# Causal masks of the score maxima in an attention and mixture-of-experts kernel: from TensorE to GpSimd, by way of copies in SBUF

## The chip, the core and the metric

The kernel runs on one core of a Trainium2 chip. The metric is the time of one execution on the device in microseconds (us), the median of several runs. A smaller time is better. All lines (L472 and the like) are lines of the kernel before, unless the text says that they are of the changed kernel.

## The reference, cut to what matters

Eight batches of 256 tokens with 256 features go through an attention layer (32 query heads of 8 features, in groups of 4 over 8 key heads, rotary positions, causal) and then through a mixture of experts with 8 routed experts, of which each token takes 2, and 2 shared experts. Both have a layer norm before and after, and a residual. The part that the change touches is the causal softmax:

```
scores = einsum('bkgtd,bksd->bkgts', qg, k) / sqrt(hd)
scores = where(causal, scores, -inf)
attn   = softmax(scores, axis=-1)
ctx    = einsum('bkgts,bksd->bkgtd', attn, v)
```

A softmax subtracts the largest score of each query before the exponential. The kernel therefore computes the scores twice: once with the queries on the partitions, only to find the maxima, and a second time with the keys on the partitions, with the maxima subtracted inside the matmul, for the exponentials. The change concerns the first of these, the pass for the maxima.

## The kernel before, in words

A batch has two tiles of 128 tokens (tt = 0 and 1). For each batch the kernel normalises x, transposes it, projects it to queries, keys and values (`project`, L342), splits the rotated queries and keys into high and low parts on GpSimd (`split`, L379), and brings keys and queries into their transposed layouts through PSUM (`keysT`, L404, whose copy out of PSUM is L423 and L425; `queriesT`, L436). `keys_apart` (L427) then spreads the keys by DMA.

**The pass for the maxima** (`maxima_of` L450, `maxima` L461). With queries of tile tt on the partitions, the keys that can be seen are the first (tt+1)*128. A score tile in PSUM holds at most 512 columns: for tt = 0 there are ten tiles (eight of 3 heads x 128 columns, two of 2 query groups x 2 heads x 128), for tt = 1 sixteen of 512 columns (2 heads x 256, or 2 groups x 1 head x 256). Each score matmul (L472) is followed by a second one (L479) that adds the mask on the array: a bf16 identity as the weights, and as moving operand a bf16 triangle of 0 and -1e30, repeated for the heads, into the last 128 columns of each head, which are those on the diagonal. That is 32 score matmuls and 32 mask matmuls in a batch, 256 of each in all. VectorE then takes the negated maximum of each row out of PSUM (L486), 26 times in a batch, 208 in all. `split_shift` (L494) and `shiftT` (L501) split these maxima into two parts, transpose them, and send them by three DMAs (L516) into the extra rows of the queries.

**The second pass** (`weights_of`, L521) makes scores again (L524), ScalarE exponentiates them into one of nine buffers (`ex`, L531, L532), GpSimd zeroes the upper triangle of the diagonal tiles there (L534), and `values` (L545) multiplies with the values (L552). `softmaxed` (L564), `contextT` and `projected` follow, then the norms and the residual (L619 to L629).

**The experts.** `tokensT`, `logits`, `first_choice`, `second_choice`, `places`, `shares` and `scatter` (L645 to L764) choose two experts for each token. `scatter` issues four indirect DMAs from GpSimd for a batch (L754), each after a small multiplication (L748) that needs `den` (L714) from VectorE. The shared experts (`shared_gate_up` L802 with L780, `shared_down` L820 with L793) are spread through the attention as work for TensorE between the other matmuls. After the attention come the routed experts, block by block.

**The order of the work.** All of the attention is put on one line of time by hand: `at(when, step, ...)` (L299) gives each step a place in units of one batch, and the sorted list is issued in that order (L1200). Each engine works through its own instructions in that order. Batch b's maxima stand at b-0.98 and the following places, 0.032 apart (L1097 to L1103), batch b's second pass from b to b+0.98, and the projection of batch b+1 and the scatter of batch b-2 fall between the maxima of batch b: the maxima of tile 1 of batch b lie beside the `split`, `keysT` and `queriesT` of tile 1 of batch b+1 and the `scatter` of batch b-2.

**PSUM buffers.** Score tiles of both passes, gate-up and down tiles share five (`ps_mm`, L115). All transposes and small projections share two (`ps_tp`, L116), used in turn: a tile there can be written when the one two before it has been read.

Of the kernel before, what the change touches and what calls it, by code (L numbers as in the profile page):

```python
# [10 lines left out]
F32 = mybir.dt.float32  # L11
F32R = mybir.dt.float32r
BF16 = mybir.dt.bfloat16
I32 = mybir.dt.int32
AF = mybir.ActivationFunctionType
ALU = mybir.AluOpType
# [3 lines left out]
P = 128  # L20
EPS = 1e-5
NEG = -1e30
HD = 8
HB = 32
SHIFT = 96
SQ = 32
EB = 256
# [3 lines left out]
def attn_moe_kernel(  # L31
# [47 lines left out]
    nc = tc.nc  # L79
    B, T, D = x.shape  # L80
# [10 lines left out]
    ISC = IS // P  # L91
    G = 4
    NKV = NH // G
    NK = NKV * HD
    NC = NKV // G
    J = 3
    NS = -(-NKV // J)
# [5 lines left out]
    RW = 4  # L103
# [9 lines left out]
    small = ctx.enter_context(tc.tile_pool(name="small", bufs=4))  # L113
    shared_pool = ctx.enter_context(tc.tile_pool(name="shared", bufs=1))
    ps_mm = ctx.enter_context(tc.tile_pool(name="ps_mm", bufs=5, space=PSUM))  # L115
# [3 lines left out]
    aconst = early.enter_context(tc.tile_pool(name="aconst", bufs=1))  # L119
    work = early.enter_context(tc.tile_pool(name="work", bufs=2))  # L120
# [7 lines left out]
    NREG = -(-NSLOT // (16 * EB)) * 16  # L128
# [12 lines left out]
    for w, lo, n in ((wq, 0, D), (wk, D, NK), (wv, D + NK, NK)):  # L141
        nc.scalar.dma_start(
            out=wqkv[:, :, lo : lo + n], in_=w.rearrange("(k p) n -> p k n", p=P)
# [3 lines left out]
    for b in range(1, B):  # L147
# [9 lines left out]
    mask = aconst.tile([P, P], BF16, name="mask")  # L157
    nc.gpsimd.memset(mask, 0.0)
    nc.gpsimd.affine_select(
        out=mask,  # L160
        in_=mask,
        pattern=[[-1, P]],
        compare_op=ALU.is_ge,
        fill=NEG,
        base=0,
        channel_multiplier=1,
    )
    ident_b = aconst.tile([P, P], BF16, name="ident_b")
# [8 lines left out]
    for sign, base in ((1, 0), (-1, 1)):  # L177
        nc.gpsimd.affine_select(
            out=place1[SHIFT:P],
            in_=place1[SHIFT:P],  # L180
            pattern=[[-2 * sign, J], [0, 1]],
            compare_op=ALU.is_ge,
            fill=0.0,
            base=base,
            channel_multiplier=sign,
# [27 lines left out]
    def set_up_router():  # L213
        nonlocal order, ones, before, upto, region0, fills, blocks, cum, unused

        order = const.tile([P, NSEL], F32, name="order")
        for e in range(NSEL):
            nc.gpsimd.memset(order[:, e : e + 1], float(NSEL - e))


        ones = const.tile([P, P], BF16, name="ones")
        before = const.tile([P, P], BF16, name="before")
        nc.gpsimd.memset(ones, 1.0)
        nc.gpsimd.affine_select(
            out=before,
            in_=ones,
            pattern=[[1, P]],
            compare_op=ALU.is_gt,
            fill=0.0,
            base=0,  # L230
            channel_multiplier=-1,
        )
        upto = const.tile([P, 2 * NSEL, 2 * NSEL], F32, name="upto")
        nc.gpsimd.memset(upto, 1.0)
        nc.gpsimd.affine_select(
            out=upto,
            in_=upto,
            pattern=[[1, 2 * NSEL], [-1, 2 * NSEL]],
            compare_op=ALU.is_ge,
            fill=0.0,  # L240
            base=0,
            channel_multiplier=0,
        )

        def counter(name, *pattern, base=0):
            sizes = [n for _, n in pattern]
            i = const.tile([P, *sizes], I32, name=f"{name}_i")
            nc.gpsimd.iota(i, pattern=[*map(list, pattern)], base=base, channel_multiplier=0)
            f = const.tile([P, *sizes], F32, name=name)
            nc.vector.tensor_copy(f, i)  # L250
            return f

        region0 = counter("region0", (NTOK, NSEL))

        fills = counter("fills", (-P, 2), (EB, NTOK // EB - 1), base=EB + P)
        blocks = counter("blocks", (1, NBLK - NSEL))
        cum = const.tile([P, NT + 1, NSEL], BF16, name="cum")
        nc.vector.memset(cum[:, 0, :], 0.0)


        unused = aconst.tile([NREG, EB, RW], I32, name="unused")
        nc.gpsimd.memset(unused, 0)
        nc.gpsimd.iota(
            unused[:, :, 1], pattern=[[1, EB]], base=NTOK, channel_multiplier=0
        )
        nc.gpsimd.memset(records, 0)
        nc.gpsimd.iota(
            records[:, :, :, 0], pattern=[[P, NT], [0, 2]], base=0, channel_multiplier=1
        )
        nc.gpsimd.iota(  # L270
            records[:, :, :, 1], pattern=[[1, NT], [0, 2]], base=0, channel_multiplier=NT
        )
# [26 lines left out]
    def at(when, step, *args):  # L299
        timeline.append((when, len(timeline), step, args))  # L300

    held = {}
# [98 lines left out]
    def heads_in(c):  # L401
        return min(J, NKV - c * J)
# [46 lines left out]

    def maxima_of(b, tt):  # L450

        width = (tt + 1) * P
        for c in range(NS):
            per = min(512 // width, heads_in(c))
            for k0 in range(0, heads_in(c), per):
                nk = min(per, heads_in(c) - k0)
                ng = 512 // (nk * width)
                for g0 in range(0, G, ng):
                    yield c, c * J + k0, nk, g0, ng

    def maxima(b, tt, c, k0, nk, g0, ng):  # L461

        qA, kst = qAs[b % 3], ksts[b % 3]
        if ("nmx", b, tt) not in held:
            held["nmx", b, tt] = small.tile(
                [P, NKV, G], F32, tag="nmx", name=f"nmx{b}_{tt}", bufs=2
            )
        nmx = held["nmx", b, tt]
        width = (tt + 1) * P
        sc = ps_mm.tile([P, ng, nk, width], F32, tag="mm", name="sc")  # L470
        for g in range(ng):
            nc.tensor.matmul(  # L472
                sc[:, g, :, :],
                lhsT=qA[0:SHIFT, c * G + g0 + g, ts(tt, P)],
                rhs=kst[0:SHIFT, k0 : k0 + nk, 0:width],
                start=True,
                stop=False,
            )
            nc.tensor.matmul(  # L479
                sc[:, g, :, width - P :],  # L480
                lhsT=ident_b,
                rhs=mask.unsqueeze(1).to_broadcast([P, nk, P]),
                start=False,
                stop=True,
            )
        nc.vector.tensor_reduce(  # L486
            nmx[:, k0 : k0 + nk, g0 : g0 + ng].rearrange("p k g -> p g k"),
            sc,
            AX.X,
            ALU.max,  # L490
            negate=True,
        )

    def split_shift(b, tt):  # L494
        nmx = held.pop(("nmx", b, tt))
        nhl = small.tile([P, NKV, 2, G], F32R, tag="nhl", name=f"nhl{b}_{tt}", bufs=2)
        nc.vector.tensor_copy(nhl[:, :, 1, :], nmx)
        nc.vector.tensor_tensor(nhl[:, :, 0, :], nmx, nhl[:, :, 1, :], ALU.subtract)
        held["nhl", b, tt] = nhl
# [21 lines left out]
    def weights_of(b, kv, s, t):  # L521
# [8 lines left out]
        )  # L530
        e = work.tile([P, G, P], F32, tag="ex", name="ex", bufs=EX)  # L531
        nc.scalar.activation(e, sc, AF.Exp, scale=QSCALE)  # L532
# [31 lines left out]
    def softmaxed(b, c, t):  # L564

        avs = held.pop(("avs", b, c, t))
        if c == 0:
            held["cx", b, t] = work.tile([P, D], F32, tag="cx", name=f"cx{b}_{t}", bufs=4)
        cx = held["cx", b, t]
        pt = ps_tp.tile([P, G, G, 32], F32, tag="tp", name="pav")  # L570
        for g in range(G):
            nc.tensor.transpose(
                pt[:, g, :, :].rearrange("p j r -> p (j r)"), avs[:, ts(g, P)], ident
            )
        rs = small.tile([P, G, G], F32, tag="rs", name="rs")
        nc.vector.reciprocal(
            rs, pt[:, :, :, HD : HD + 1].rearrange("p g j x -> p g (j x)")
        )
        nc.vector.tensor_tensor(
            cx[:, ts(c, P)].rearrange("p (j g d) -> p g j d", j=G, g=G),  # L580
            pt[:, :, :, 0:HD],
            rs.unsqueeze(3).to_broadcast([P, G, G, HD]),
            ALU.mult,
        )
# [472 lines left out]
        )  # L1057


    EX = 9  # L1060
    at(0.6, clear_slots)
    at(0.7, clear_sums)
    for i in range(PIECES):
# [1 line left out]
    for i, a in enumerate((-2.2, -0.93, 0.03)):  # L1065
        at(a, clear_operands, i)
        at((-1.7, a, a)[i], set_ones, i)
        at((-1.97, -0.96, 0.02)[i], clear_values, i)
    at(0.5, set_up_router)
    at(-2.3, norm1, 0)  # L1070
    at(-2.3, normed1, 0)
# [10 lines left out]
    for b in range(B):  # L1082
# [14 lines left out]
        when = b - 0.98  # L1097
        for tt in range(TT):
            for m in maxima_of(b, tt):
                at(when, maxima, b, tt, *m)  # L1100
                when += 0.032
            at(when + 0.001, split_shift, b, tt)
            at(when + 0.07, shiftT, b, tt)  # L1103
        last = b == B - 1
        parts_of = [(c, t) for c in range(NC) for t in range(TT)]
        when, unit = b, 0.98 / (NC * 3 * G)
        if b == 0:
            parts_of.sort(key=lambda part: part[1])
            when, unit = -0.4, 0.04
        for c, t in parts_of:  # L1110
            if b == 0 and t > 0:
                when = max(when, 0)
# [222 lines left out]
```

## Time and profile before

| what | value |
|---|---|
| runs | 822.48, 825.74, 825.18 us; median 825.18 |
| the profiled execution | 821.22 us, its span 819.5 us, mean granted TensorE clock 0.975 |
| TensorE (PE) busy | 757.0 us, 3977 matmuls |
| VectorE (DVE) busy | 490.6 us |
| ScalarE (ACT) busy | 250.6 us |
| GpSimd (POOL) busy | 347.8 us |
| score matmuls L472 | 256, 99.5 us busy, mean 419 ns |
| mask matmuls L479 | 256, 73.2 us busy, mean 288 ns |
| maxima L486 | 208, 129.0 us busy, mean 641 ns |

PE is the row of the matmuls and PEld that of their weight loads, which overlap. Matmuls are pipelined: the row of one shows it from its start to its modelled end, and the next one starts before that end, so busy times of TensorE count the same moment twice and its cost is better read from the distance between the ends of neighbours. A matmul of f32 data with f32 weights stands in the trace as two records (a gate-up tile of four matmuls as x8), one of the types float32r or bf16 as one. The first 20 us set the kernel up, the attention lasts until about 500 us, and the routed experts take the rest.

### The profile page before, as it was taken

The page shows a single profiled execution, that of the slowest core. Times are in us where ns is not written, and L with a number is a line of the kernel's source. Part 1 is how long each engine was busy: PE and PEld are TensorE (multiplying, and loading weights), DVE is VectorE, ACT ScalarE, POOL GpSimd, SP SyncE. Part 2 cuts the span into 40 slices and gives each one's busy share as a digit, 9 for nine tenths or more (in the row PEclk, how much of TensorE's full clock was granted, in tenths as well). Part 3 has the DMA queues.
Part 4 walks back from the last instruction along what each step waited for, and adds up shares of the span by engine and source line. Part 5 has one row for each costly group of instructions (what it writes and reads, how often), then busy time and mean ns, then how long its engine had stood idle before and what let it go on. Part 6 is the DMA issues. An engine that isn't in the chain of part 4 may idle for free. (4 is left out here: it accounts for less than half of the span.)

```text
span 819.5 us, 11843 instructions
## 1 busy us (share of the span) xinstructions
PE 757.0 (92%) x3977; PEld 575.8 (70%) x3977; DVE 490.6 (60%) x1409; ACT 250.6 (31%) x550; POOL 347.8 (42%) x622
## 2 busy tenths in 40 slices
PE   4979799999999999999999998799999999999981
PEld 3535466766766766766766667688888888888961
DVE  5756777667667667667675636366564656442234
ACT  3554444234234334334334422021111111111213
POOL 4567545435435436436233432334233443443224
PEclk9899999999999999999999999899999999999986
DMA  5023300000000000000000005265655757577343
GB/s 155 6 85 90 89 16 16 7 22 16 8 23 16 7 21 16 8 22 16 7 22 3 19 8 203 52 229 157 203 163 179 225 158 228 167 220 279 57 118 102
DMA packets 30994, 70.41 MB, mean 86 GB/s; under 512 B 8544, under 2 KB 25440, under 8 KB 28240
## 3 DMA queue, kind: packets, MB, share of 16 engines
q1 hardware_dynamic: 19488, 54.23, 19.1%
q0 software_dynamic: 8128, 9.77, 6.4%
q10 hardware_dynamic: 3312, 5.60, 2.3%
q8 instruction: 33, 0.54, 0.3%
q14 instruction: 33, 0.27, 0.1%
HBM read 55.16 MB, written 11.80 MB: 82 GB/s over the span
## 5 line engine op out<-in xcount | busy, mean ns | idle before, releaser
L780 PE MATMUL gu<-xgT,w 128*128 128x256 f32 (+1 forms) x840 | 163.9, 354 | 1.0 <-ACT xgT L981 0.7
L780 PE MATMUL gu<-x2T,ws_sb 128*128 128x256 f32 x640 | 155.4, 390 | 3.9 <-PEq L1241 3.8
L780 PEld LDWEIGHTS gu<-xgT,w 128*128 128x128 f32 x840 | 144.5, 190 | 18.1 <-ACT xgT L981 1.0
L532 ACT ACTIVATE ex<-scT 128x512 f32<-128x512 f32 x192 | 113.6, 597 | 136.2 <-PE scT L524 123.7
L486 DVE TENSOR_REDUCE nmx<-sc 128x2 f32<-128x512 f32 (+2 forms) x208 | 129.0, 641 | 24.1 <-PE sc L479 23.8
L780 PEld LDWEIGHTS gu<-x2T,ws_sb 128*128 128x128 f32 x640 | 121.4, 195 | 26.1 <-issue 5.0
L534 POOL TENSOR_SCALAR_AFFINE_SELECT ex<-ex 128x512 f32<-128x512 f32 x128 | 81.1, 639 | 113.5 <-ACT ex L532 113.4
L1017 POOL DMA_INDIRECT sums<-yb,of x37 | 58.5, 1582 | 109.5 <-DVE yb L1016 71.7
L472 PE MATMUL sc<-kst,qA 96*128 96x512 f32 (+2 forms) x256 | 99.5, 419 | 0.7 <-issue 0.5
L524 PE MATMUL scT<-qA,kst 102*128 102x512 f32 x192 | 96.2, 509 | 1.8 <-DMA qA<-nm 1.8
L1006 ACT ACTIVATE sg<-gu 128x256 f32<-128x256 f32 (+1 forms) x105 | 37.6, 358 | 191.1 <-PE gu L780 177.8
L994 DVE STREAM_TRANSPOSE xgT<-xg 32x128 f32<-32x128 f32 x240 | 72.6, 303 | 29.9 <-DMA xg<-rows,of 21.1
L793 PE MATMUL po<-w,act 128*128 128x256 f32 x370 | 83.1, 379 | 0.0
L793 PE MATMUL po<-ws_sb,sact 128*128 128x256 f32 x320 | 74.6, 390 | 4.5 <-DVE sact L816 4.5
L793 PEld LDWEIGHTS po<-w,act 128*128 128x128 f32 x370 | 69.8, 190 | 9.2
L793 PEld LDWEIGHTS po<-ws_sb,sact 128*128 128x128 f32 x320 | 61.5, 195 | 18.2 <-DVE sact L816 4.9
L479 PE MATMUL sc<-mask,ident_b 128*128 128x256 bf16 (+2 forms) x256 | 73.2, 288 | 0.0
L1007 DVE TENSOR_TENSOR act<-sg,gu 128x256 f32<-128x256 f32 (+1 forms) x105 | 38.7, 387 | 56.3 <-ACT sg L1006 55.7
L815 DVE SCALAR_TENSOR_TENSOR th<-th,gu 128x256 f32<-128x256 f32 x70 | 29.3, 418 | 65.6 <-ACT th L814 65.6
L935 POOL DMA_INDIRECT xg<-rows,of x37 | 35.9, 970 | 62.4 <-DMA of<-slots 47.6
L472 PEld LDWEIGHTS sc<-kst,qA 96*128 96x128 f32 x256 | 50.3, 197 | 13.5 <-issue 3.6
L552 PE MATMUL av<-ex,v_aug 128*32 128x512 f32 x384 | 58.5, 605 | 1.3 <-POOL ex L534 1.3
(171 smaller groups left out, 839.9 us busy)
## 6 DMA issues: line engine op xcount, KB each, us to landing
w<-in_routed SPq DMA_DIRECT2D x21, 1920.0 KB
ws_sb<-in_shared ACTq DMA_DIRECT2D x8, 480.0 KB
xs<-in_x SPq DMA_DIRECT2D x8, 256.0 KB
rows<-x2n SPq DMA_DIRECT2D x8, 256.0 KB
acc<-sums SPq DMA_DIRECT2D x4, 512.0 KB
sums<-ya SPq DMA_DIRECT2D x14, 128.0 KB
kst<-kA SPq DMA_DIRECT2D x16, 96.0 KB
out<-acc SPq DMA_DIRECT2D x2, 512.0 KB
```

The costliest lines, as they stand in the source:

```text
L472: nc.tensor.matmul(sc[:, g, :, :], lhsT=qA[0:SHIFT, c * G + g0 + g, ts(tt, P)], rhs=kst[0:SHIFT, k0 : k0 + nk, 0:width], start=True, stop= ...
L479: nc.tensor.matmul(sc[:, g, :, width - P :], lhsT=ident_b, rhs=mask.unsqueeze(1).to_broadcast([P, nk, P]), start=False, stop=True,)
L486: nc.vector.tensor_reduce(nmx[:, k0 : k0 + nk, g0 : g0 + ng].rearrange("p k g -> p g k"), sc, AX.X, ALU.max, negate=True,)
L524: nc.tensor.matmul(sc, lhsT=ksts[b % 3][0:KR, kv, ts(s, P)], rhs=qAs[b % 3][0:KR, ts(kv // J, G), ts(t, P)], start=True, stop=True,)
L532: nc.scalar.activation(e, sc, AF.Exp, scale=QSCALE)
L534: nc.gpsimd.affine_select(out=e, in_=e, pattern=[[0, G], [1, P]], compare_op=ALU.is_ge, fill=0.0, base=0, channel_multiplier=-1,)
L552: nc.tensor.matmul(av[32 * j : 32 * j + 32, :], lhsT=v_aug[b % 3 * TT + s][:, c * G + j, :], rhs=e.rearrange("p g t -> p (g t)"), start=(s ...
L780: nc.tensor.matmul(gu[:, half, :], lhsT=m[:, k, ts(i, P)], rhs=xT[:, k, :], start=(k == 0), stop=(k == KC - 1),)
L793: nc.tensor.matmul(po, lhsT=act[:, k, ts(t, P)], rhs=d[:, k, :], start=(k == 0), stop=(k == ic - 1),)
L994: nc.vector.transpose(to[ts(j, SQ), :, :, ts(i, SQ)], of[ts(i, SQ), :, :, ts(j, SQ)])
L1007: nc.vector.tensor_tensor(act[:, i, :], sg, gu[:, 1, :], ALU.mult)
L1017: put = nc.gpsimd.indirect_dma_start(out=sums, out_offset=bass.IndirectOffsetOnAxis(ap=of[:, t, 1:2], axis=0), in_=y, in_offset=None, comp ...
```

## The change

For batches 0 and 1 the mask stays on the array. From batch 2 on (`BY_POOL = 2`) it leaves: the score tile of a diagonal block is copied by ScalarE from PSUM to one of five SBUF buffers (`sm`), GpSimd sets the upper triangle to -1e30 there with `affine_select`, and VectorE takes the maxima from SBUF. Score tiles are now always 128 keys wide for each head, for all batches; tile 1 has its off-diagonal block (kt = 0) and its diagonal block (kt = 1) in separate tiles, whose two maxima are combined by one more small VectorE instruction in `split_shift`. The places of the steps are new: tiles stand 0.026 apart (0.024 from batch 2 on), the select of a diagonal tile comes 0.03 and its maximum 0.07 after its matmul, and `split_shift` moves behind that. To make room in SBUF, `ex` has 8 buffers instead of 9 and `cx` 3 instead of 4, and the table `unused` takes the place of the buffer of the shared experts' activations, which is first written later.

```diff
-        unused = aconst.tile([NREG, EB, RW], I32, name="unused")
+        unused = shared_pool.tile([P, ISC, T], F32, tag="sact", name="unused")
+        unused = unused[0:NREG].rearrange("p i t -> p (i t)")[:, 0 : EB * RW].bitcast(I32)
...
     def maxima_of(b, tt):
-        width = (tt + 1) * P
-        for c in range(NS):
-            per = min(512 // width, heads_in(c))
-            for k0 in range(0, heads_in(c), per):
-                nk = min(per, heads_in(c) - k0)
-                ng = 512 // (nk * width)
+        for kt in range(tt + 1):
+            for c in range(NS):
+                nk = heads_in(c)
+                ng = 1 if kt == tt and b >= BY_POOL else 512 // (nk * P)
                 for g0 in range(0, G, ng):
-                    yield c, c * J + k0, nk, g0, ng
+                    yield kt, c, g0, ng
 
-    def maxima(b, tt, c, k0, nk, g0, ng):
+    def scores(b, tt, kt, c, g0, ng):
...
+        sc = ps_mm.tile([P, ng, nk, P], F32, tag="mm", name="sc")
+        by_array = kt == tt and b < BY_POOL
         for g in range(ng):
             nc.tensor.matmul(
                 sc[:, g, :, :],
                 lhsT=qA[0:SHIFT, c * G + g0 + g, ts(tt, P)],
-                rhs=kst[0:SHIFT, k0 : k0 + nk, 0:width],
+                rhs=kst[0:SHIFT, c * J : c * J + nk, ts(kt, P)],
                 start=True,
-                stop=False,
+                stop=not by_array,
             )
...
+        if kt == tt and not by_array:
+            sm = work.tile([P, ng, nk, P], F32, tag="sm", name="sm", bufs=SM)
+            nc.scalar.copy(sm, sc)
+            sc = sm
+        held["sc", b, tt, kt, c, g0] = sc
+
+    def masked(b, tt, kt, c, g0, ng):
+        sm = held["sc", b, tt, kt, c, g0]
+        nc.gpsimd.affine_select(
+            out=sm,
+            in_=sm,
+            pattern=[[0, ng * heads_in(c)], [-1, P]],
+            compare_op=ALU.is_ge,
+            fill=NEG,
+            base=0,
+            channel_multiplier=1,
+        )
...
     def split_shift(b, tt):
-        nmx = held.pop(("nmx", b, tt))
+        both = held.pop(("nmx", b, tt))
+        nmx = both[:, 0]
+        for kt in range(tt):
+            nc.vector.tensor_tensor(nmx, nmx, both[:, kt + 1], ALU.min)
...
-    EX = 9
+    EX, SM, BY_POOL = 8, 5, 2
...
-                at(when, maxima, b, tt, *m)
-                when += 0.032
+                at(when, scores, b, tt, *m)
+                delay = 0
+                if m[0] == tt and b >= BY_POOL:
+                    at(when + 0.03, masked, b, tt, *m)
+                    delay = 0.07
+                at(when + delay, maxima, b, tt, *m)
+                when += 0.026 if b < BY_POOL else 0.024
+            when += delay
```

By instruction, in a batch from 2 on: 36 score matmuls (24 of 384 columns and 12 of 256) and no mask matmul, against 32 and 32; 24 new copies on ScalarE and 24 new selects on GpSimd (16 of 384 columns and 8 of 256); 34 maxima and one minimum on VectorE, against 26 maxima. Batches 0 and 1 have 36 score matmuls, 24 mask matmuls, 30 maxima and the minimum.

This is how the built program of the changed kernel stands on two engines around the scatter of a batch (that of batch 3, beside the maxima of tile 1 of batch 5; in words, and only what bears on the order). GpSimd:

```
select of an ex tile, two splits of the projection's queries
records, scatter DMA, records, scatter DMA         (wait for den of VectorE)
select of sm tile 1
split of queries (2 instructions)
records, scatter DMA, records, scatter DMA
select of sm tile 2
split, select of sm tile 3, split, select of sm tile 4, split, selects 5 and 6, split, selects 7 and 8, ...
```

VectorE:

```
den
two products of a gate-up tile
maximum of sm tile 1                                (waits for select 1)
copy of the values' sums out of PSUM
maximum of sm tile 2                                (waits for select 2)
two products of a gate-up tile
copies of the transposed keys out of PSUM (kA)
maxima of sm tiles 3 and 4, ...
```

On TensorE the first query transposes of tile 1 (`queriesT`, c = 0) take the `ps_tp` buffer of the transposed keys and wait, in both kernels, for the copy kA.

## The prediction, made before the changed kernel ran

> **What bounds the kernel now.** I read the page first: TensorE is busy for 757.0 of 819.5 us, the others for 31 to 60%.
>
> ```profile
> PE 757.0 (92%) x3977; PEld 575.8 (70%) x3977; DVE 490.6 (60%) x1409; ACT 250.6 (31%) x550; POOL 347.8 (42%) x622
> ```
>
> Then the busy time by windows, cut at the first query transposes of tile 1 of batches 4 to 7, so that each row is one batch of the steady state.
>
> ```profile
> core 0: us, PE busy (x) PEld busy (x) DVE busy (x) ACT busy (x) POOL busy (x), PEclk, DMA share, GB/s
> 189.86:251.91 62.05, 60.89 (x345) 43.78 (x345) 42.98 (x122) 22.93 (x50) 28.86 (x63) 1.00 0.06 15
> 251.91:314.11 62.20, 61.03 (x345) 43.78 (x345) 43.26 (x122) 22.99 (x50) 29.12 (x63) 1.00 0.05 15
> 314.11:376.36 62.25, 61.06 (x345) 43.80 (x345) 43.28 (x121) 23.27 (x49) 29.18 (x63) 1.00 0.06 15
> ```
>
> A batch takes 62.2 us, of which TensorE is idle for 1.2; VectorE is busy for 43.3, GpSimd for 29.1, ScalarE for 23. So TensorE sets the pace, and work taken from it counts, as long as nobody makes it wait. Whether somebody does is a question of places, not of averages. The timeline of GpSimd around a batch's scatter:
>
> ```profile
> 309.07 0.19 POOL L748 TENSOR_TENSOR records<-m,den 128x1 f32<-128x1 f32 x1 [0.85 <-DVE den L714]
> 309.79 1.08 POOL L754 DMA_INDIRECT slots<-records,to  x1 [0.53 <-POOL records L748]
> 310.90 0.20 POOL L748 TENSOR_TENSOR records<-m,den 128x1 f32<-128x1 f32 x1
> 311.38 0.98 POOL L754 DMA_INDIRECT slots<-records,to  x1 [0.28 <-POOL records L748]
> 312.37 0.27 POOL L398 CAST qs<-full 128x96 fp32r<-128x96 f32 x1
> 312.73 0.39 POOL L399 TENSOR_TENSOR qs<-full,qs 128x96 fp32r<-128x96 f32 x1
> 313.08 0.19 POOL L748 TENSOR_TENSOR records<-m,den 128x1 f32<-128x1 f32 x1
> ...
> 316.04 0.27 POOL L398 CAST qs<-full 128x96 fp32r<-128x96 f32 x1
> ```
>
> Here GpSimd has hardly a gap from 309.1 to 319.2, and none over 0.5 us. VectorE and the transposes on TensorE, in the same stretch:
>
> ```profile
> 313.36 0.41 DVE L423 CAST kA<-pkT 96x256 fp32r<-96x256 f32 x1
> 313.69 0.27 DVE L425 CAST kA<-pkT 64x128 fp32r<-64x128 f32 x1
> ```
> ```profile
> 314.11 0.53 PE L441 MATMUL pqT<-ident_r,qs 128*96 128x128 f32 x4
> 317.51 0.56 PE L441 MATMUL pqT<-ident_r,qs 128*96 128x128 f32 x4
> ```
>
> TensorE's transposes start 0.15 us after kA has left PSUM (313.69 + 0.27 = 313.96), and the next group 0.06 us after the queries that GpSimd finished at 317.45. Both leave TensorE no slack: what delays kA delays TensorE.
>
> **What TensorE loses.** The timeline of TensorE (start, duration):
>
> ```profile
> 312.15 0.45 PE L472 MATMUL sc<-kst,qA 96*128 96x512 f32 x1
> 312.44 0.28 PE L479 MATMUL sc<-mask,ident_b 128*128 128x256 bf16 x1
> 312.48 0.48 PE L524 MATMUL scT<-qA,kst 102*128 102x512 f32 x1
> 312.79 0.40 PE L472 MATMUL sc<-kst,qA 96*128 96x512 f32 x1
> 313.03 0.29 PE L479 MATMUL sc<-mask,ident_b 128*128 128x256 bf16 x1
> ```
>
> The ends are at 312.60, 312.72, 312.96, 313.19 and 313.32: a mask of 256 columns moves the end by 0.12 to 0.13, a score of 512 by 0.235, whether a mask or a score stood before it. Elsewhere in the same view masks of 384 and 128 columns move it by 0.18 and 0.075, scores of 384 and 256 by 0.18 and 0.12 (0.165 for 256 behind a 128-column mask). Per batch, masks: 8 x 0.18 + 16 x 0.125 + 8 x 0.075 = 4.04. Scores before: 8 x 0.18 + 4 x 0.12 + 12 x 0.235 + 8 x 0.165 = 6.06; after: 24 x 0.18 + 12 x 0.12 = 5.76. TensorE loses 4.34 us per batch, 26.0 for batches 2 to 7; batches 0 and 1, with 16 masks of 384 and 8 of 256 columns, lose 0.16 + 0.30 each, 0.9 together.
>
> By the row of L479 it would be far more: 73.2 x 6/8 = 54.9 us. [...] By the row the forecast would be some 765 us; by the ends it cannot be below 819.5 - 26.9 = 792.6. I take the ends.
>
> **What the others gain, per batch.** ScalarE: 24 copies. Its nearest rows out of PSUM are 370 ns (L332, 256 columns) and 580 (L448, 512): 0.475 for 384, so 16 x 0.475 + 8 x 0.37 = 10.6 us, 33.6 in all. GpSimd: 24 selects. The row L534 has 639 ns for 512 columns; for 384 the bounds are 0.48 (in proportion) and 0.64 (no less than for 512), I take 0.53, and 0.42 for 256 (0.32 to 0.64): 11.8 us, 40.9 in all. VectorE: rows 682 ns for 512 columns and 549 for 384 give 0.416 for 256, so 24 x 0.549 + 8 x 0.416 + 2 x 0.682 = 17.9 against 8 x 0.549 + 18 x 0.682 = 16.7, and 0.2 for the minimum: 44.7. Each fits in 58 us (62.2 - 4.3).
>
> [...]
>
> The smaller edits cost nothing on the path: `unused` is free well before the activations are written (places 0.6 and 1.5); an `ex` tile lives about 0.21 places of 0.041 each, five to six of 8 buffers; `cx` needs two of three. If their cover were gone, ScalarE or VectorE would wait on values or context, and that would show as waits of L532 and L579.
>
> **The new waits.** Select 1 stands behind the first two scatter DMAs on GpSimd, select 2 behind all four; VectorE waits for select 2 before the maximum, and queued behind that are the products of a gate-up tile and kA. With den's end at 308.99 as zero: the first pair ends at 3.4 (312.36), select 1 at 3.9, the split at 4.6, the second pair (2.96 long) at 7.6, select 2 at 8.1. VectorE then needs 0.55 for the maximum, 0.80 for the products and 0.60 for kA, as in the rows: 10.05, and TensorE's transposes start at 10.2. Before, they started at 314.11, at 5.1. den itself comes 0.4 later, since one more maximum of 384 columns stands ahead of it. From the gate-up tile before the choice of experts, which VectorE waits for in both kernels, the transposes come 5.5 us later. In this stretch TensorE would have lost 0.66 of the 4.34; the rest, 3.7, counts. A batch gets 5.5 - 3.7 = 1.8 us longer, for batches 2 to 6, in which projection and scatter both lie beside the maxima: +9.0. Batch 7 has no projection beside it, but VectorE and the gate-up tiles wait as well: between -4.3 and 0, I take -2. Batches 0 and 1: -0.9. Two smaller waits: the last select of tile 0 now lies behind the norm's power (0.72 us) on GpSimd and before the tokens' transposes, and the maxima's DMA starts 0.13 places closer to its reader. Their bounds are 0 and about 1 us per batch; 0.5 for five batches is +2.5.
>
> Sum: 9.0 - 2 - 0.9 + 2.5 = +8.6. The profiled execution, 821.22 with 1.7 us around its span, would be about 830; the median of the runs is 4 us above it, so 825.2 + 8.6 = 834.
>
> **Rivals.** (a) Faster: the averages decide. If the distances of 0.03 and 0.07 (4.4 us) are enough and the scatter costs TensorE 1 us per batch, it is -26.9 + 5 = -22: 803. For it: every engine has 13 us or more free per batch. Against it: kA and the queries have no slack today. (b) Half: VectorE comes to den earlier, or a select takes 0.48, and the delay is 2 to 3 us instead of 5.5: -1.0 per batch, some 820. (c) Much slower: the five buffers. ScalarE's copy 6 waits for maximum 1 and copy 7 for maximum 2, and the exponentials queue behind them; with 3 us more for six batches, +18 on top: 852. This decides if VectorE lags more than five tiles (0.12 places, 7.5 us) behind TensorE.
>
> **How the numbers follow.** The scatter delay 0.48, faster 0.24, half 0.18, much slower 0.10. The likeliest case alone spans 826 to 845 (delay 4.5 to 7.5 us); over the cases 803 to 848. Differences under 0.5% (4.1 us) cannot be told from no change: faster 0.29 (all of (a), a third of (b)), same 0.15, slower 0.56.
>
> **What would show it.** TensorE's busy time falls by 20 us or more, while its idle time in a batch from 2 on grows from 1.2 to about 7 us, in one gap before L441's counterpart for tile 1, with kA late; VectorE waits about 3 us each for selects 1 and 2; a batch takes 63 to 64 us. I am wrong if the transposes start within 3 us of their old distance from den, if the selects stand ahead of the scatter in time, or if the gap is elsewhere.

## The result and the profile after

The changed kernel takes 866.91 us (median of four runs, 864.66 to 868.44) and the kernel before 824.88 us beside it: the ratio is 1.0506, with a 95% interval of 1.0479 to 1.0532. The profiled execution has a span of 864.3 us and a mean granted clock of 0.943, against 819.5 us and 0.975. The forecast was 834 and its range ended at 848.

Lines below are those of the changed kernel: L470 is the score matmul, L487 ScalarE's copy, L493 the select, L510 the maximum, L443 the query transposes, L425 and L427 the copies of kA, L741 den, L775 and L781 the scatter, L551 the score matmul of the second pass, L588 and L599 the context's copy `avs` and its transposes `pav`, L807 a gate-up tile.

The page, with the busy time by engine and, of the span in 40 slices, the granted clock of TensorE in tenths:

```profile
PE 761.3 (88%) x3801; PEld 589.3 (68%) x3801; DVE 496.0 (57%) x1473; ACT 298.3 (35%) x694; POOL 411.3 (48%) x766
PEclk8899888998998999899899999899999999999977
```

The last of these rows for the kernel before:

```profile
PEclk9899999999999999999999999899999999999986
```

TensorE does 176 records less and is busy for 4 us more. Its clock, which before stood at 9 or above from the third slice to the end of the attention, now falls to 8 again and again.

Busy times by windows, one row for each batch, cut as before at the first query transposes of tile 1 (batches 4 to 5 and 5 to 6; after the width come busy time and, in brackets, records of PE, PEld, DVE, ACT and POOL, then the granted clock):

```profile
207.91:276.17 68.26, 60.09 (x317) 44.83 (x317) 43.74 (x131) 31.09 (x73) 39.66 (x87) 0.95 0.05 14
276.17:344.42 68.25, 60.11 (x316) 44.81 (x317) 43.72 (x131) 31.09 (x73) 39.63 (x87) 0.95 0.05 14
```

A batch takes 68.25 us instead of 62.2. TensorE is idle for 8.1 of them (1.2 before), and its clock, 1.00 before, is 0.95.

The stretch that the prediction worked through, in the timelines of GpSimd, VectorE and TensorE (start, duration, and in brackets the idle time ahead and what ended it); den's end is at 334.32:

```profile
336.70 0.98 POOL L781 DMA_INDIRECT slots<-records,to  x1 [0.28 <-POOL records L775]
337.71 0.53 POOL L493 TENSOR_SCALAR_AFFINE_SELECT sm<-sm 128x384 f32<-128x384 f32 x1
...
340.85 0.99 POOL L781 DMA_INDIRECT slots<-records,to  x1 [0.28 <-POOL records L775]
341.86 0.53 POOL L493 TENSOR_SCALAR_AFFINE_SELECT sm<-sm 128x384 f32<-128x384 f32 x1
```
```profile
338.27 0.55 DVE L510 TENSOR_REDUCE nmx<-sm 128x3 f32<-128x384 f32 x1 [3.19 <-POOL sm L493]
...
342.42 0.55 DVE L510 TENSOR_REDUCE nmx<-sm 128x3 f32<-128x384 f32 x1 [3.00 <-POOL sm L493]
...
344.00 0.27 DVE L427 CAST kA<-pkT 64x128 fp32r<-64x128 f32 x1
```
```profile
339.48 0.66 PE L599 MATMUL pav<-ident,avs 128*128 128x128 f32 x4 [1.09 <-DVE avs L588]
339.89 0.48 PE L551 MATMUL scT<-qA,kst 102*128 102x512 f32 x1
344.42 0.87 PE L443 MATMUL pqT<-ident_r,qs 128*96 128x128 f32 x4 [4.05 <-DVE kA L427]
345.09 2.02 PE L807 MATMUL gu<-x2T,ws_sb 128*128 128x256 f32 x4
```

This is the predicted chain: select 1 stands behind the first pair of DMAs and select 2 behind both, VectorE waits 3.19 and 3.00 us, and the transposes start 10.1 us after den (forecast 10.2, before 5.1). What the prediction had no term for is in the last row: four records of a gate-up tile take 2.02 us, where eight take 1.89 at full clock (at 335.65 in the same trace). Busy times by windows again, this time cut at the places where the granted clock changes, 3.41 us apart:

```profile
336.40:339.82 3.42, 2.33 (x15) 1.81 (x14) 1.15 (x2) 1.46 (x3) 2.76 (x7) 1.00 0.02 1
339.82:343.25 3.43, 0.55 (x4) 0.23 (x2) 0.83 (x2) 0.19 (x1) 3.01 (x7) 1.00 0.02 1
343.25:346.66 3.41, 2.24 (x8) 2.00 (x9) 3.02 (x9) 1.37 (x3) 3.15 (x10) 0.50 0.25 49
346.66:350.08 3.42, 3.42 (x12) 2.79 (x11) 0.78 (x3) 1.23 (x4) 1.01 (x3) 0.50 0.14 30
350.08:353.49 3.41, 3.41 (x20) 2.85 (x19) 2.03 (x6) 2.40 (x7) 1.25 (x4) 1.00 0.00 0
```

After a window in which TensorE was busy for only 0.55 us, two windows have the clock 0.50. In the second of them TensorE has no gap, but 12 records take the time of 20. Five batches have such a place: 6.83 us at half clock from 138.45, 206.72, 274.99, 343.25 and 411.52.

**Where 44.8 us of span come from.** Cut at the first query transposes of tile 1: up to batch 2, -1.4; from batch 2 to batch 3, +14.5 (57.45 us instead of 42.99); the four batches from there to batch 7, +22.4; the rest, batch 7's second pass and the routed experts, +9.3. In one batch (68.25 against 62.25): idle time 8.14 against 1.19, +7.0; of 6.83 us at half clock TensorE works in 5.66 (the first 1.17 still belong to the gap), which costs half of that, +2.8; its own work at full speed is then 60.11 - 2.83 = 57.3 against 61.06, -3.8. The sum is +6.0. The split between the last two is an estimate: the kernel of experiment 7 does the same matmuls of a batch in 58.02 us at a clock of 1.00, which makes it +2.1 and -3.0. Over the attention from 30 us on, TensorE works for 48.7 us at half clock, and for none before; by the same reckoning that is at most 24 of the 44.8 us.

### The profile page after: what moved, and what is told of

It reads as the page before. It is cut to its first block, busy times and chain, and to the rows that moved or that the text cites. A ratio compares the mean times of both kernels' runs of the same rounds, so it can differ in the third digit from the quotient of the medians.

```text
span 864.3 us, 11992 instructions
## 1 busy us (share of the span) xinstructions
PE 761.3 (88%) x3801; PEld 589.3 (68%) x3801; DVE 496.0 (57%) x1473; ACT 298.3 (35%) x694; POOL 411.3 (48%) x766
## 5 line engine op out<-in xcount | busy, mean ns | idle before, releaser
L807 PE MATMUL gu<-x2T,ws_sb 128*128 128x256 f32 x640 | 168.0, 413 | 6.4 <-PEq L1274 3.6
L807 PE MATMUL gu<-xgT,w 128*128 128x256 f32 (+1 forms) x840 | 163.9, 354 | 1.0 <-ACT xgT L1008 0.7
L807 PEld LDWEIGHTS gu<-xgT,w 128*128 128x128 f32 x840 | 144.5, 190 | 18.1 <-ACT xgT L1008 1.0
L807 PEld LDWEIGHTS gu<-x2T,ws_sb 128*128 128x128 f32 x640 | 129.1, 208 | 28.7 <-issue 6.3
L559 ACT ACTIVATE ex<-scT 128x512 f32<-128x512 f32 x192 | 113.6, 603 | 71.4 <-PE scT L551 64.7
L470 PE MATMUL sc<-kst,qA 96*128 96x384 f32 (+1 forms) x288 | 105.0, 406 | 1.7 <-DMA kst<-kA 1.3
L510 DVE TENSOR_REDUCE nmx<-sm 128x3 f32<-128x384 f32 (+1 forms) x144 | 69.5, 500 | 48.9 <-POOL sm L493 48.6
L551 PE MATMUL scT<-qA,kst 102*128 102x512 f32 x192 | 90.5, 485 | 0.3 <-ACT ex L559 0.3
L470 PEld LDWEIGHTS sc<-kst,qA 96*128 96x128 f32 x288 | 58.7, 208 | 35.0 <-issue 11.8
L487 ACT COPY sm<-sc 128x384 f32<-128x384 f32 (+1 forms) x144 | 62.4, 453 | 58.1 <-PE sc L470 32.7
L510 DVE TENSOR_REDUCE nmx<-sc 128x3 f32<-128x384 f32 (+1 forms) x120 | 65.9, 581 | 16.8 <-PE sc L470 11.8
L493 POOL TENSOR_SCALAR_AFFINE_SELECT sm<-sm 128x384 f32<-128x384 f32 (+1 forms) x144 | 68.2, 483 | 10.8 <-ACT sm L487 10.5
```

What stands on the lines that cost most here:

```text
L470: nc.tensor.matmul(sc[:, g, :, :], lhsT=qA[0:SHIFT, c * G + g0 + g, ts(tt, P)], rhs=kst[0:SHIFT, c * J : c * J + nk, ts(kt, P)], start=Tru ...
L487: nc.scalar.copy(sm, sc)
L493: nc.gpsimd.affine_select(out=sm, in_=sm, pattern=[[0, ng * heads_in(c)], [-1, P]], compare_op=ALU.is_ge, fill=NEG, base=0, channel_multip ...
L510: nc.vector.tensor_reduce(nmx[:, kt, c * J : c * J + heads_in(c), g0 : g0 + ng].rearrange("p k g -> p g k"), held.pop(("sc", b, tt, kt, c, ...
L551: nc.tensor.matmul(sc, lhsT=ksts[b % 3][0:KR, kv, ts(s, P)], rhs=qAs[b % 3][0:KR, ts(kv // J, G), ts(t, P)], start=True, stop=True,)
L807: nc.tensor.matmul(gu[:, half, :], lhsT=m[:, k, ts(i, P)], rhs=xT[:, k, :], start=(k == 0), stop=(k == KC - 1),)
```

## The experiments

**Theory:** in GpSimd's queue two selects stand behind the scatter's DMAs, VectorE waits for them and holds kA, TensorE is idle for 4 us, and for this the clock then runs at half. **Rivals:** the five buffers and ScalarE's copies; masks in SBUF or the 128-wide tiles as such; and, for the clock, that it costs nothing or is not from the gap. Ratios are to the kernel before, on the same chip, with the 95% interval.

**1. All but the mask's move.**

```diff
-    EX, SM, BY_POOL = 8, 5, 2
+    EX, SM, BY_POOL = 8, 5, 8
```

> All of the change except the mask's move: 128-wide score tiles, maxima by block, EX = 8, cx = 3, the table's new buffer, but the mask stays on the array for all eight batches. Theory (GpSimd's queue makes kA late, then TensorE's clock halves): no selects of scores, so no gap over 1 us before the query transposes and no half clock in the attention; the tiles themselves save about 0.45 us a batch by the ends of the matmuls, so some 821, 818 to 828. Rival (the tiles or the smaller edits cost the time, for instance 24 maxima of 384 columns for VectorE, or too few buffers): 840 or more.

830.25 us, 1.0044 (1.0028 to 1.0061). This is above the expectation of 818 to 828, but far from 840. No gap before the transposes is left. The four batches take 63.3, 63.4, 64.2 and 65.5 instead of 62.2; in the second TensorE is idle for 2.5, in waits under 1 us (maxima and context in a new order on VectorE), and in the attention the clock is at half for 6.83 us at 89 and 3.41 at 376. So the tiles cost about 3 us, not the 42.

**2. The scatter behind the selects.**

```diff
-            at(a + 0.39 + 0.03 * t, scatter, b, t)
+            at(a + 0.68 + 0.03 * t, scatter, b, t)
```

> The changed kernel with the four scatter DMAs 0.29 places later, behind the last select of the tile instead of among the selects. Theory: selects 1 and 2 no longer wait, VectorE's waits of 3.2 and 3.0 us and the 4.05 us gap before the transposes go, with them the 6.83 us of half clock; a batch takes 58 to 61 us instead of 68.3, the time is 795 to 815. Rival (five buffers and ScalarE's copies hold the exponentials, or masks in SBUF are slow as such): the batch stays above 64 us, 845 or more.

849.13 us, 1.0249 (1.0207 to 1.0291): 18 us less than the changed kernel, but far from the 795 to 815 expected; the total even lies where the rival had it (845 or more), so only the trace tells them apart. The 4 us gap and the 6.83 us of half clock are gone, and a batch takes 62.8 to 64.7 us. But the DMAs now stand ahead of selects of the exponentials on GpSimd, for which TensorE waits 12.9 us in all (11 waits of `av`; the three longest, 1.82, 2.30 and 2.64, in batch 7's second pass), and waits of 1.45 us, behind VectorE's reading of the projection, still bring 3.41 us of half clock to three of four batches. The stage from batch 2 to batch 3 stays at 53 us.

**3. kA past VectorE.**

```diff
-        copied = copier(b - 1)
+        copied = nc.scalar.copy
```

> The changed kernel with the scatter where it is, but kA copied out of PSUM by ScalarE in all batches, so that kA no longer queues behind VectorE's wait for select 2. Theory: TensorE loses by kA alone; the transposes start about 5 us after den, without the gap of 4.05 us, though VectorE still waits some 3 us each for selects 1 and 2. If nothing else on TensorE waits for VectorE then, a batch takes 60 to 62 us and the time is 805 to 825; if the wait passes to avs and the gate-up products, a gap of 2 to 4 us comes behind it and the time is 835 to 860. Rival (the five buffers): ScalarE's copy 6 or 7 stands ahead of exponentials, TensorE waits for ex, 850 or more.

852.12 us, 1.0300 (1.0268 to 1.0332). The gap before the transposes is gone though VectorE waits as before, so it was kA that carried the delay. But a batch takes 65.0 us: TensorE now waits for the gate-up products and the context that stand behind VectorE's wait (1.16 and 0.96 us at 336.4 and 338.5), and 3.41 us of half clock follow. This is the second case of the expectation by its time, with several waits of about 1 us in place of one gap of 2 to 4. The time is also in the rival's range (850 or more), but TensorE waits for exponentials (`ex`) only 1.8 us in the whole attention.

**4. The wait alone, in the kernel before.** The mask stays on the array; VectorE only has to wait for GpSimd's queue once per batch, ahead of kA:

```diff
             at(a + 0.39 + 0.03 * t, scatter, b, t)
+        at(a + 0.421, mark, b)
+        at(a + 0.472, await_mark, b)
...
+    def mark(b):
+        held["mark", b] = small.tile([P, 1], F32, tag="mark", name="mark", bufs=2)
+        nc.gpsimd.memset(held["mark", b], 0.0)
+
+    def await_mark(b):
+        seen = small.tile([P, 1], F32, tag="seen", name="seen", bufs=2)
+        nc.vector.tensor_copy(seen, held.pop(("mark", b)))
```

> The kernel before, masks on the array, with the wait alone: GpSimd clears one column behind the last scatter DMA, and VectorE copies that column ahead of kA. Theory: the transposes come 8 to 9.5 us after den instead of 5.1, TensorE has one gap of 3 to 4.5 us in each of five batches, and its clock is granted at half for 6.83 us behind it; five times (3.5 + 3.4) makes 855 to 865. If the wait costs its own length and no more: 840 to 846. If TensorE makes it up from work queued elsewhere: 825 to 830.

861.54 us, 1.0424 (1.0404 to 1.0444), the first of the three cases. From its timelines of VectorE and TensorE, and the windows at the changes of the clock (L773 is the new copy; the other lines are those of the kernel before):

```profile
337.21 0.15 DVE L773 COPY seen<-mark 128x1 f32<-128x1 f32 x1 [4.02 <-POOL mark L769]
```
```profile
338.82 0.87 PE L441 MATMUL pqT<-ident_r,qs 128*96 128x128 f32 x4 [3.80 <-POOL qs L398]
```
```profile
334.12:337.53 3.41, 0.90 (x7) 0.58 (x6) 0.32 (x2) 1.16 (x2) 2.73 (x8) 1.00 0.01 1
337.53:340.94 3.41, 2.12 (x8) 1.88 (x9) 2.76 (x8) 0.58 (x1) 1.90 (x7) 0.50 0.19 42
340.94:344.36 3.42, 3.42 (x10) 2.19 (x8) 0.66 (x2) 0.38 (x1) 0.00 (x0) 0.50 0.18 40
```

A copy of one column makes VectorE wait 4.02 us and TensorE 3.80 here (the name in the bracket is not the one to trust: this group's queries were split by 334.1, and kA ended at 338.67), at five places (2.66 to 4.44 us), and a batch takes 67.6 to 68.6 us. No mask has moved and no score tile is copied, and yet the time is 34 us longer: the wait alone is enough. That the batch is as long as in the changed kernel is in part chance. Here TensorE is idle for 4.8 us of a batch; in the changed kernel it is idle for 8.1, of which some 3 lie in further waits, and these are about what the missing mask matmuls save.

**5. More work in the gap.** TensorE gets 14 score matmuls more in five batches, in front of the last tile before the gap (L553 below; L560 is the kernel's own):

```diff
         sc = ps_mm.tile([P, G, P], F32, tag="mm", name="scT")
+        if 1 <= b <= 5 and (kv, s, t) == (2 * G - 1, 0, 1):
+            for _ in range(14):
+                nc.tensor.matmul(
+                    sc,
...
```

> The changed kernel with more work for TensorE: in batches 1 to 5 of the second pass, 14 extra score matmuls (14 x 0.235 = 3.3 us, their results overwritten) stand in front of the last score tile before the gap of 4.05 us, so the array is busy while it would wait for kA. Theory (the idle time in a window of 3.41 us halves the clock of the next one): the gap shrinks to 0.5 to 1 us, the half clock behind it is gone in batches 4 to 7, kA comes when it came; a batch takes 65 to 66 us instead of 68.3 (5.7 us at half clock no longer cost 2.8), the time is 850 to 857, less than the changed kernel's 867 for 70 matmuls more. Rival (the half clock is not from the gap, or costs nothing): 866 or more.

855.43 us, 1.0360 (1.0329 to 1.0392), where the changed kernel has 867. With 70 matmuls more it is some 12 us shorter. TensorE in its timeline, and a batch by windows:

```profile
334.74 3.42 PE L553 MATMUL scT<-qA,kst 102*128 102x512 f32 x14
337.99 0.39 PE L560 MATMUL scT<-qA,kst 102*128 102x512 f32 x1
339.27 0.53 PE L443 MATMUL pqT<-ident_r,qs 128*96 128x128 f32 x4 [0.89 <-DVE kA L427]
```
```profile
273.70:339.27 65.57, 61.94 (x330) 46.25 (x331) 43.89 (x131) 30.96 (x74) 39.77 (x87) 0.97 0.05 14
```

kA comes no sooner: the transposes start 10.1 us after den, as in the changed kernel. What the matmuls buy is the clock, and the gate-up tile behind them takes 1.94 us for its eight records. A batch takes 65.6 instead of 68.25 us, 2.7 less. That this is so near to the 2.8 worked out above is chance: the half clock behind the gap is gone and the wait of 1.09 us for `avs` too, but 3.41 us of half clock (hence the 0.97) have come up at another place, behind the 1.45 us wait for `rb`, and TensorE works in 3.36 of them, which costs 1.7.

**6. Six buffers.** `EX, SM` are 7 and 6 instead of 8 and 5.

> The changed kernel with six buffers for the scores instead of five, and seven for the exponentials instead of eight. Theory: VectorE's wait for selects 1 and 2 stays, so the gap before the transposes and the time stay: 862 to 870. Rival (the five buffers hold ScalarE, whose copies stand 25 us before maxima, and the exponentials behind them): the gaps get shorter by a tile, 855 or less.

869.78 us, 1.0536 (1.0496 to 1.0576). ScalarE's waits for maxima, 11.4 us between 200 and 400 us in the changed kernel, are gone from the list of waits, and the gap of 4.05 us is where it was. Rival (c) of the prediction falls.

**7. The DMAs apart.** `scatter` gets an argument for which of its two DMAs it issues, and each is a step:

```diff
-            at(a + 0.39 + 0.03 * t, scatter, b, t)
+            for k in range(2):
+                at(a + 0.39 + 0.1 * (2 * t + k), scatter, b, t, (k,))
```

> The changed kernel with each scatter DMA a step of its own, 0.1 places (6 us) apart, the first where it was. Theory: no select stands behind more than one DMA (1.5 us), less than the 2.5 us between a select and its maximum, so VectorE's two 3 us waits go and no window of 3.41 us has 1.5 us of idle TensorE in batches 4 to 7; a batch takes 60 to 62 us. The half clocks of batch 2's stage (103 to 120 us) stay, which has another cause: 822 to 836 in all. Rival (masks in SBUF cost TensorE its pace in any order): a batch stays at 64 us or more, 845 or more.

840.33 us, 1.0177 (1.0143 to 1.0210): 27 us less than the changed kernel from the order of four DMAs, 4 us above the expectation. A batch takes 61.7 to 63.2 us; one without half clock:

```profile
198.26:260.21 61.95, 58.02 (x317) 42.90 (x317) 44.81 (x131) 31.01 (x74) 39.91 (x87) 1.00 0.06 15
```

VectorE's longest wait for a select is 1.7 us, and TensorE's longest before the transposes in these batches 1.5. Two windows of 3.41 us at half clock are left, at 313.97 and 375.41, where none was expected; both lie behind waits of 1.45 us for `rb`. The stage of batch 2 takes 54 us, with 6.83 + 17.07 us of half clock between 88.7 and 119.4, as expected from the other runs.

**8. From the fourth batch on.** As 7, with BY_POOL = 3.

> As the kernel with the DMAs spread, and the mask stays on the array for batch 2 too (from the fourth batch on it leaves). Theory: the stage between the transposes of batches 2 and 3 takes 43 to 47 us as with the mask on the array, instead of 53 to 57, since GpSimd no longer sets the pace where TensorE has no shared experts' work; 812 to 826. Rival (that stage is slow for the tiles, not for GpSimd): no gain on the kernel with the DMAs spread alone.

830.19 us, 1.0056 (1.0019 to 1.0094). The stage takes 46.1 us instead of 54. There the selects of tile 0 share GpSimd with splits, powers and residuals, while TensorE has no shared experts' work that would fill the time; where the first gap comes, at 103 us, the scatter has not begun. It is a second place where selects wait in GpSimd's queue and VectorE with kA behind them (in experiment 7 TensorE's gap for kA is 3.38 us there, at 103.70), this time without a DMA. The time is 4 us over the expectation, since the batches still take 60.5 to 63.1.

**9 and 10. Two small moves against the gaps that are left,** on the kernel of experiment 8, and the same alone on the kernel before:

```diff
-        at(a + 0.302, second_choice, b)
+        at(a + 0.32, second_choice, b)
...
-                at(a + 0.22, keysT, b, tt)
+                at(a + 0.19, keysT, b, tt)
```

> The mask leaves the array from the fourth batch on with the scatter DMAs spread, and two small moves against the gaps left there: the second choice of experts 0.018 places later, so that VectorE reads the projection out of PSUM first (it ended 1.45 us of idle before the context transposes), and the keys' transposes 0.03 places earlier, so that kA stands ahead of two maxima that wait for selects (0.97 and 0.49 us of idle). Theory: idle time per batch falls from 3.7 to under 1.5 us, no half clock in batches 4 to 7, a batch takes 59 to 60 us, 815 to 823, below the kernel before. Rival (the idle time moves to another wait): a batch stays at 61 us or more, 827 to 832.

> The kernel before, masks on the array, with the same two small moves alone. Theory: its only gap of that kind, 0.99 us per batch, goes, nothing else: 820 to 824. It tells how much of the other kernel's gain is these moves and how much the mask's move. Rival: the gap is hidden elsewhere, 825 to 828.

Both missed: 835.28 us, 1.0094 (1.0057 to 1.0131), and 837.03 us, 1.0112 (1.0072 to 1.0152). The waits for kA and `rb` do go. But the matmul of `places` needs the second choice, and TensorE's queue comes to it before VectorE does: a new wait of 2.64 us per batch in one, 1.90 in the other, and one of 1.72 and 2.35 us for the earlier keys' transposes at 81 us. The kernel before is as sensitive as the changed one: two steps moved by one or two microseconds cost it 1.1%.

**11. One DMA less to wait for.** As 4, but VectorE waits for the third DMA of the four.

> The kernel before with the wait on VectorE one DMA shorter (1.5 us): it waits for the third of the four scatter DMAs, not the fourth. Theory: the gap before the transposes is 2 to 2.7 us instead of 3.8 and still over the idle time in one window of 3.41 us from which the next one runs at half (1.5 us in the runs so far), unless a window's edge cuts it into two smaller parts: 3.4 us of half clock behind most of the gaps, a batch takes 64 to 66.5 us, the time is 840 to 852. Rival (only a gap over 3 us halves the clock): no half clock there, a batch takes 63.3 to 64 us, 832 to 837.

838.41 us, 1.0118 (1.0067 to 1.0169), between the two ranges, 840 to 852 and 832 to 837: the five gaps are 2.97, 2.10, 2.34, 2.33 and 1.18 us, and the half clock behind them is 6.83, 3.41, 3.41, none and none. The third and the fourth gap, by windows at the grid of the clock:

```profile
263.00:266.39 3.39, 1.33 (x9) 0.73 (x7) 1.30 (x5) 1.19 (x2) 2.74 (x7) 1.00 0.02 1
266.39:269.80 3.41, 3.14 (x10) 2.72 (x11) 1.78 (x5) 0.58 (x1) 2.29 (x9) 0.50 0.35 78
```
```profile
327.83:331.24 3.41, 2.22 (x15) 1.42 (x13) 0.87 (x3) 1.58 (x3) 2.75 (x8) 1.00 0.01 1
331.24:334.66 3.42, 2.28 (x13) 1.97 (x13) 2.61 (x8) 0.58 (x1) 3.08 (x9) 1.00 0.25 51
334.66:338.07 3.41, 3.41 (x22) 2.78 (x21) 2.42 (x6) 1.88 (x5) 0.71 (x2) 1.00 0.14 32
```

Two gaps of the same length: the first lies almost whole in one window, which has 2.06 us of idle time, and the next one runs at half; the edge cuts the second into 1.19 and 1.14 us, and the clock stays.

**12. From the fourth batch on, with two other moves.** The kernel of experiment 8, with the keys' transposes earlier from batch 4 on only, and the context transposes moved instead of the choice:

```diff
-                at(a + 0.22, keysT, b, tt)
+                at(a + (0.22 if b < 4 else 0.19), keysT, b, tt)
...
-            a = when + (0.1 if last else 0.12)
+            a = when + (0.1 if last else 0.15 if (c, t) == (0, 1) else 0.12)
```

> The mask leaves the array from the fourth batch on with the scatter DMAs spread, the keys' transposes 0.03 places earlier from batch 4 on (the part of the last attempt that took its wait away), the second choice back in its place, and instead the context transposes of the first half of the heads, tile 1, 0.03 places later, behind VectorE's reading of the projection. Theory: the gap of 1.45 us and those of kA go, none over 1.2 us is left in batches 4 to 7, no half clock there; a batch takes 59 to 60.5 us, 816 to 824, some 5 us below the kernel before. Rival (each move of VectorE's or TensorE's work makes another wait): a gap of 1.5 us or more at another line, 827 or more.

822.12 us against 827.08 for the kernel before, 0.9942 (0.9918 to 0.9966), inside the expected 816 to 824. Two of its batches by windows:

```profile
186.72:247.08 60.36, 58.33 (x317) 42.96 (x316) 44.66 (x131) 30.80 (x74) 39.77 (x87) 1.00 0.06 15
247.08:308.08 61.00, 58.47 (x318) 43.02 (x316) 44.18 (x131) 30.91 (x74) 39.76 (x87) 1.00 0.06 15
```

The clock is 1.00 and a batch takes 60.4 to 61.0 us, a little above the 59 to 60.5 expected. TensorE is busy for 2.6 us less per batch than before, and idle for 0.8 to 1.3 us more. Up to batch 7's first transposes this kernel is 7 us ahead of the kernel before (369.09 against 376.36); from there to the end it takes 452.1 us against 443.2, since the waits of the last stage are still in it. So five microseconds is what the version gains, not what the mask's move alone is worth: the kernel before with the same two moves was not run.

## Why the prediction failed

- **The bound, the order on GpSimd, VectorE's two waits, kA's delay:** right, the times to 0.2 us. The transposes came 10.1 us after den (10.2), behind select 2, as forecast. ("None over 0.5 us" of GpSimd's gaps was a small misreading: the line shown has 0.53.) Maxima out of SBUF were priced like those out of PSUM, and so they were: 548 ns for 384 columns in the rows of L510, 553 out of PSUM.
- **The step that failed: "A batch gets 5.5 - 3.7 = 1.8 us longer".** It priced a gap at its length. The clock of the work behind the gap then also stood at 0.50, which cost 2.1 to 2.8 us per batch: the largest part of the 4.2 us by which a batch came out longer than forecast (6.0 instead of 1.8). It is also why the sign "TensorE's busy time falls by 20 us or more" did not come: 761.3 us against 757.0. The rows before showed a clock of 1.00 in each batch and no gap over 1 us; the prediction left the clock there and had neither a term nor a rival for it. The trace before has such a place, at the end of the attention: TensorE waits 2.54 us for the norm ahead of L652, with a gap of 0.20 behind it; 1.77 us of idle time lie in the window from 498.69 to 502.10, and in the next 3.41 us, at a clock of 0.50, TensorE works through 9 records, in the 3.41 us after them through 21 at 1.00. By this one place the gap of 4 us would have been priced, as an estimate, at one window at half or more, 1.7 us at least.
- **Idle time:** forecast from 1.2 to about 7, "in one gap", measured 8.1, of which the one gap is 4.05. The rest lies in the waits for `avs`, which queued behind VectorE's first wait (1.09), for kA of tile 0 (0.95), for `rb` (1.45 instead of 0.99) and for an exponential (0.34). That the total is near is in part luck: the "two smaller waits" of the prediction, at 0.5, were others.
- **The masks:** 4.34 us per batch forecast by the ends of the matmuls; 3.0 to 3.8 by the account above, and 2.6 in the last kernel (58.4 us busy against 61.0). It was too much, but the row's 54.9 us for six batches, 9.2 each, would have been far off.
- **"for batches 2 to 6":** batch 2 is not like the others. Up to batch 3 a stage has 43 us and no shared experts' work for TensorE, so waits for GpSimd's selects set its pace: +14.5 where 1.8 was forecast. With the DMAs apart it still took 54 us, and keeping that batch's masks on the array gave 8 of them back (10 us in all, 840 to 830).
- **"I take -2" for the end:** +9.3, of which 7.3 come before the attention's last projection (123.5 us from batch 7's first transposes instead of 116.2). It is the same chain once more: at 469.55 VectorE has waited 3.97 us for a select behind two of the scatter's DMAs, `avs` queues behind it, and TensorE waits 3.38 us (the line is below this list); 3.41 us of half clock follow. With the masks on the array in the same tiles (experiment 1) this stretch takes 116.2 us. What the last 2 us in the routed experts come from stays open.
- **The rivals:** "averages decide" (803) needed every engine's work in the right order, and the best of the twelve other versions here reached 822. "Five buffers" (852) came nearest to the measured 867, but not by its cause, which fell with experiment 6.

TensorE in the changed kernel, in batch 7's second pass:

```profile
471.54 0.66 PE L599 MATMUL pav<-ident,avs 128*128 128x128 f32 x4 [3.38 <-DVE avs L588]
```

## What to carry to other kernels

When TensorE is the bound and its clock is at 1.00, do not price a new wait at its length alone: here one of 4.05 us had 6.83 us at a clock of 0.50 behind it, which cost 2.1 to 2.8 us more, and waits of 1.45 us in experiment 2 had 3.41 us at half. Look at how much idle time falls into one window of the clock (3.41 us here), not only at the longest gap. Before a step goes onto an engine with an ordered queue, list what stands ahead of it there: four DMA issues of some 1.5 us each decided this change, and setting them apart won back 27 us. The saving of 3.0 to 3.8 us per batch on the bounding engine was smaller here than the price of one such wait, 4.05 us and the half clock behind it.

## What the runs showed of the hardware

The clock's changes lie on a fixed grid of 3.413 us in every trace here (111.15, 138.45 and 206.72 in the changed kernel: 8 and 20 steps apart). Over all fourteen traces, from 30 to 510 us, with the idle time taken between the records of the matmuls (some records can be missing, so the edges are soft and a count can shift by one or two), a window at full clock was followed by

| idle time of TensorE in the window | next window full | next window half |
|---|---|---|
| under 1.4 us | 1733 | 3 |
| 1.4 to 1.8 us | 10 | 23 |
| 1.8 us and more | 1 | 54 |

So in these traces 1.4 to 1.8 us of idle time in a window had half clock behind them in 23 of 33 cases and 1.8 us or more in 54 of 55, in one gap (2.34 us in experiment 11) or in several (1.16 and 0.96 in experiment 3), and where a gap lies on the grid decides too (2.34 and 2.33 us in experiment 11, of which only the first had half clock behind it). Of the windows at half clock, all 25 with 0.8 us or more of idle time were followed by another one at half. In the changed kernel and in experiments 4 and 6 the five half clocks begin just 20 steps apart (68.27 us, as from 206.72 to 274.99), in experiment 3 four of them 19 steps (64.85 us, from 144.68 on). A batch seems to fall into step with the grid. Why was not tested, but the sums above then tell where a batch's time goes, and not what it would take with one wait less. A gap of 1.45 us, with small ones beside it, had a window at half behind it (at 317.12 and 381.39 us in experiment 2).
